# Re-ordering the loads and the work of the first batch element in a graph-network kernel

## The chip, the cores and the metric

The kernel runs on one core of a Trainium2 chip. The metric is the device time of one execution in microseconds (us). Before the change three runs took 2395.70, 2395.92 and 2396.19 us, median 2395.92 us. The profile is one further execution, of 2396.57 us, whose span from the first to the last instruction is 2394.8 us; the remaining 1.8 us lie outside the instructions.

## What is computed

There are 16 batch elements with 1024 nodes of 128 features and a 1024 x 1024 matrix `adj` each. Two residual blocks follow one another:

```python
# layer 0
degree = adj.sum(axis=-1)[:, :, None]
s   = einsum('bid,bij->bjd', x, adj) / degree
x   = layernorm(x + relu(concat([x, s]) @ W.T + b))
# layer 1: four GNN layers, each
src_agg = einsum('bjv,bij->biv', nodes @ ws + bs, adj / row_norms)
dst_agg = einsum('bjv,bji->biv', nodes @ wd + bd, adj / column_norms)
nodes   = tanh(concat([src_agg, nodes @ wn + bn, dst_agg]) @ wu + bu)
# then x = layernorm(x + nodes)
```

The norms are the square roots of the sums of squares of the rows and columns. Layers 2 and 3 read concatenated earlier features, so that their weights have two and three blocks of 128 rows.

## The kernel before, in words

Elements are worked off one after another (loop `for b in range(B)`, L1242). While TensorE multiplies for one element, the next one's matrix is loaded, squared, scaled and transposed beside it. This is possible for every element but the first, which has a stage of its own ahead of the loop (L1047 to L1236). The change touches that stage and the first pass of the loop (`if b == 0`).

The order of the instructions on each engine is the order of the program text (L1041 switches off any other scheduling). Each DMA issue is written on a named queue: `nc.sync` (the profile's SP), `nc.gpsimd` (POOL) or `nc.scalar` (ACT). Transfers of SP and ACT signal their landing on eight completion semaphores in rotation, so that an issue waits until the previous user of its semaphore has landed. POOL has eight of its own.

**Loads (L1063 to L1085).** `w0n` is the first layer's weight, `xn` holds x in two halves of nodes (h = 1 first), `a` the matrix in four "pairs" of row blocks (`PAIRS`), and each pair comes in four pieces, one for each group `g` of 32 partitions, 256 KB a piece. Before, SP issues `w0n`, groups 0 and 1 of both halves of x and groups 0 and 1 of all pairs; POOL issues groups 2 and 3 of all of them. SP then issues the small bias `b0c`, and for the four layers the weights (`fetch_weights`, L180) with four biases of 512 bytes each (L192), mixed with four blocks of transposed-to-be matrix rows (`load_rows`).

**First stage (L1182 to L1229).** TensorE transposes `w0` and x (`to_xT`), starts the sum of x and y in PSUM by a product of x with the identity (`with_x`), and multiplies x by its half of `w0` (`weights_of_x`). When a pair of row blocks has landed, `squares_of` takes the squares on ScalarE and the degrees on VectorE, and `gathers_of` makes four products of x with the matrix on TensorE. The sums are scaled (`scaled`), multiplied by the other half of `w0` and passed through relu into `yT` (`weights_of_agT`). `with_y` transposes y by products with the identity that accumulate onto x in PSUM. `norm_stats` reads that sum on VectorE and takes a power on GpSimd; half 1 is written by ScalarE (`norm_write_act`), half 0 by VectorE (`norm_write`), and `to_x1` transposes the result, a copy on ScalarE following.

Between these steps lie the weight foldings: since the layers are linear, `fold_begin` (transposes of three weights, their copies, and products of the biases) and `fold_end` (products of the transposed weights with `wu`, and their copies) merge `ws`, `wd`, `wn` with `wu`. They use two PSUM buffers in turn (`small`, L241), so a third waits for the copy of the first. Before, layer 0 and 1 are folded in the first stage, layer 1 with its transposes copied by VectorE and its bias copies held back (`biases`, L1222 and L1226) until ScalarE has written half 1 of the norm and copied its transpose.

**First layer of element 0 (L1259 to L1306).** `messages` makes four groups of products; functions in `between` are called after groups 0, 1, 2. `plain_layer` then makes 34 products of 512 columns: two of the node's own weights (`z`), sixteen with the matrix (`d`), sixteen with its transpose (`z`). `hooks` names what is issued ahead of which product. Before, layer 2 is folded at hooks 5 and 8, layer 3 at 9 and 12, and the sums of layer 2's weights are in `second0` at hook 11.

Of the kernel before, what the change touches and what calls it, by code (L numbers as in the profile page):

```python
# [8 lines left out]
F32 = mybir.dt.float32  # L9
# [5 lines left out]
P = 128  # L15
# [8 lines left out]
def adj_resnorm_kernel(ctx: ExitStack, tc: tile.TileContext, x, adj, w0, b0, layers, out):  # L24
# [152 lines left out]

        return wm if l in PAIRED else wm[:, :KEPT[l] * 2 * P].rearrange("p (c v) -> p c v", v=2 * P)

    def fetch_weights(raw, l, q, wm=None):  # L180
# [9 lines left out]
        bc = raw.take(4)  # L190
        for k, v in enumerate((bs, bd, bn, bu)):
            q.dma_start(bc[:, k:k + 1], v.rearrange("(p o) -> p o", o=1))  # L192
# [48 lines left out]
    def small(name, shape=(K,)):  # L241
        return ps_s.tile([P, *shape], F32, tag="small", name=name)
# [220 lines left out]
    def norm_stats(pn, blks, name, shifted=False):  # L463


        n = len(blks)
        stats = one.tile([P, BPH, 6], F32, tag="stats", name=f"st{name}")
        mv = two.tile([P, BPH, 2], F32, tag="mv", name=f"mv{name}")
        for q in range(n):
            nc.vector.bn_stats(stats[:, q], pn[:, blks[q]])  # L470
            nc.vector.bn_aggr(mv[:, q], stats[:, q])
        ve = two.tile([P, BPH], F32, tag="ve", name=f"ve{name}")
        nc.vector.tensor_scalar_add(ve[:, :n], mv[:, :n, 1], LN_EPS)
        rstd = two.tile([P, BPH], F32, tag="rst", name=f"rs{name}")
# [13 lines left out]
    def norm_write_act(dst, pn, stats, q):  # L488
        _, rstd, shift = stats
        nc.scalar.activation(dst, pn, AF.Identity, bias=shift[:, q:q + 1], scale=rstd[:, q:q + 1])  # L490
# [563 lines left out]
    def load_pair(q, pair, groups):  # L1054
        h, k = pair
# [3 lines left out]
    def load_nodes(q, h, groups):  # L1059
        for g in groups:  # L1060
            q.dma_start(xn[g * C:(g + 1) * C, h * BPH:(h + 1) * BPH], xv[h][g])

    nc.sync.dma_start(w0n, w0)  # L1063
    shares = ((nc.sync, range(G // 2)), (nc.gpsimd, range(G // 2, G)))
    for h in (1, 0):
        for q, groups in shares:
            load_nodes(q, h, groups)
    make_identity(nc, ident)
    for pair in PAIRS:
        for q, groups in shares:  # L1070
            load_pair(q, pair, groups)
    nc.sync.dma_start(b0c, b0.rearrange("(p o) -> p o", o=1))
    raw = Raw()
    wm = message_tile("wm1_0")
    Q = combined(0, "Q")
    places = {q: Q[i].rearrange("p k (u c) -> p (k u) c", u=2) for q, i in ((2, 2), (3, 3), (0, 4))}
    places[1] = one.tile([P, 2 * NJ, HW // 2], F32, tag="T2", name="rows1_0")
    rows, fetched = {}, []
    for l, q in enumerate((None, 2, 3, None)):
        fetched.append(fetch_weights(raw, l, nc.sync, None if l else wm))  # L1080
        if q is not None:
            rows[q] = load_rows(0, q, [places[q]])
    wm = as_chunks(wm, 0)
# [18 lines left out]
    pt = small("w0tr", [HW])  # L1102
    for k in range(2):
        nc.tensor.transpose(pt[:, k * P:(k + 1) * P], w0n[:, k * P:(k + 1) * P], ident)
    nc.scalar.copy(w0T.rearrange("p k v -> p (k v)"), pt[:, :2 * P])

    sq = []
    for p in (3, 4):
# [45 lines left out]
    def scaled(h):  # L1154
        nc.vector.tensor_mul(agT[:, half(h)], pa[h], dinv[:, half(h)])

    def weights_of_x(h):
        pw[h] = product(f"pw0_0_{h}")
        nc.tensor.matmul(pw[h], w0T[:, 0], xT[:, half(h)], start=True, stop=False)

    def weights_of_agT(h):
        nc.tensor.matmul(pw[h], w0T[:, 1], agT[:, half(h)], start=False, stop=True)
        nc.scalar.activation(blocks(yT[:, half(h)]), nodes(pw[h]), AF.Relu, bias=b0c)

    def with_x(h):

        pn[h] = ps_t.tile([P, BPH, P], F32, tag="pt", name=f"yn0_{h}")
        nc.tensor.matmul(pn[h].rearrange("p q d -> p (q d)"), ident, xn[:, h * BPH:(h + 1) * BPH].rearrange("p q d -> p (q d)"),
                         start=True, stop=False)

    def with_y(h):
        for q in range(BPH):
            i = h * BPH + q
            nc.tensor.matmul(pn[h][:, q], yT[:, i * P:(i + 1) * P], ident, start=False, stop=q == BPH - 1)

    def to_x1(h):
        pt = product(f"x1tr_{h}")
        for q in range(BPH):
            nc.tensor.transpose(pt[:, q * P:(q + 1) * P], x1n[:, h * BPH + q], ident)
        nc.scalar.copy(x1T[:, half(h)], pt)  # L1180

    for h in (1, 0):  # L1182
        to_xT(h)
        with_x(h)
        weights_of_x(h)
    for pair in PAIRS[:2]:
        squares_of(*pair)
        gathers_of(*pair)
    nc.vector.tensor_add(sq[6], sq[6], sq[7])
    add_square(5)  # L1190
    add_square(6)
# [1 line left out]
    degree_row(1)  # L1193
    squares_of(*PAIRS[2])
    gathers_of(*PAIRS[2])
    add_square(0)
    add_square(1)
    first, second = 2, 3
# [7 lines left out]
    gather(0, first)  # L1206
    weights_of_agT(1)
    square(first)
    square(second)
    gather(0, second)  # L1210
    add_square(first)
    with_y(1)
    scaled(0)
    weights_of_agT(0)
    stats = {1: norm_stats(pn[1], range(BPH), "0_0_1", True)}
    fold_begin(0, fetched[0])
    with_y(0)
# [12 lines left out]


    kept = scratch.tile([N, D], F32, tag="kept", name="kept0")
# [9 lines left out]
    for b in range(B):  # L1242
# [8 lines left out]
        if b == 0:  # L1251
# [13 lines left out]
            def rows0(destination, finish):  # L1265
                for q in (2, 3):
                    transpose_rows(rows[q], q, at)

            def cinv0(destination, finish):
                cinv[0] = factor_rows_now(0, 1, inv, "cinv")  # L1270

            def second0(destination, finish):
                columns0(range(NJ, NB), 1)
                sums_of_weights(2, fetched[2][3])
                weight_sums(own_seven(2, fetched[2][3]))
                nc.sync.dma_start(wsave[2], fetched[2][3])
                destination(1, cinv[0])
                columns0(range(NJ), 1)

# [380 lines left out]
```

## Time and profile before

| what | value |
|---|---|
| median of 3 runs | 2395.92 us |
| the profiled execution / its span | 2396.57 us / 2394.8 us |
| TensorE busy | 2377.7 us, 99% of the span |
| VectorE / ScalarE / GpSimd busy | 87% / 41% / 11% |
| TensorE clock granted | 1.0 throughout |
| first product with the matrix | at 13.31 us |
| first of the 34 products of element 0's first layer | at 42.45 us |

The page's shares of busy time are means over 2.4 ms, of which the changed stage is the first 60 us or so. To see that stage, ask for the busy times by stretches of time, then for the order of the instructions of one engine in such a stretch. In those rows the columns are start, duration, engine, line, operation, out<-in, shapes, count, and in brackets how long the engine was idle before and what ended it. Products in four-byte floats are two passes each, so 16 rows of `pa` are eight products.

### The profile page before, as it was taken

Reading aid. Unit: us, or ns where it says so; the run is one execution under the profiler, and the core shown is the slowest. Engines: PE = TensorE matmul, PEld = TensorE weight load, DVE = VectorE, ACT = ScalarE, POOL = GpSimd, SP = SyncE. Lnnn points to the kernel's source line nnn. Section 1 sums busy time; section 2 is a strip of 40 time slices with the busy share of each in tenths; the row PEclk is TensorE's granted clock in tenths of the full one; section 3 lists DMA queues with packets and bytes.
Section 4 is the critical chain, followed back from the end, with each engine's and each line's share of the span. In section 5 each row is a group of like instructions: output and inputs, shape, how many; then the busy total and the mean of one; then the engine's idle time right before and its main releaser. Section 6 shows DMA issues by size and latency. Waiting matters only on the chain.

```text
span 2394.8 us, 39324 instructions
## 1 busy us (share of the span) xinstructions
PE 2377.7 (99%) x15293; PEld 1288.4 (54%) x15293; DVE 2089.2 (87%) x2814; ACT 980.3 (41%) x1842; POOL 273.8 (11%) x102
## 2 busy tenths in 40 slices
PE   8999999999999999999999999999999999999998
PEld 4444554645556455554655546455464555645555
DVE  5998888999889989889988889888899888998954
ACT  5524345253343524435244452534525344352322
POOL 4101111001111011110111110111100111101110
PEclk9999999999999999999999999999999999999999
DMA  9527244262633627335272442634426253362400
GB/s 206 123 75 146 69 114 90 70 148 57 137 75 81 138 48 157 61 97 116 55 163 56 107 97 71 147 69 111 91 69 151 57 132 78 80 141 48 100 22 22
DMA packets 365897, 232.03 MB, mean 97 GB/s; under 512 B 152784, under 2 KB 336848, under 8 KB 365712
## 3 DMA queue, kind: packets, MB, share of 16 engines
q1 hardware_dynamic: 364944, 227.16, 42.6%
q0 software_dynamic: 768, 2.36, 0.4%
q8 instruction: 121, 1.98, 0.4%
q14 instruction: 64, 0.52, 0.1%
HBM read 209.59 MB, written 19.84 MB: 96 GB/s over the span
## 4 chain that ended last, share of the span: by engine, by line
PE 95%; DVE 2%; DMA 1%; SPq 1%; issue 1%; ACT 0%; POOLq 0%; DVEq 0%
PE m L1005 40%; PE z L1005 29%; PE pt L247 9%; PE pt_z L247 5%; PE m_f L583 5%; PE z_f L583 2%; PE pw L247 2%; PE m3s L1005 1%; PE z L851 1%; DMA wm<-in_L_gnn_ws_dram 1%; PE pt_p L247 1%; SPq L640 1%; DVE acc L331 0%; DMA a<-in_adj_dram 0%; PE d L851 0%
## 5 line engine op out<-in xcount | busy, mean ns | idle before, releaser
L1005 PE MATMUL m<-a,t 128*64 128x512 f32 x1008 | 434.6, 593 | 0.2 <-DVE t L711 0.2
L1005 PE MATMUL m<-at,t 128*64 128x512 f32 x1008 | 418.5, 592 | 0.0
L1005 PE MATMUL m<-Q,S 128*64 128x512 f32 x880 | 394.0, 593 | 0.0
L1005 PE MATMUL m<-T,S 128*64 128x512 f32 (+1 forms) x1040 | 393.5, 573 | 0.0
L456 POOL TENSOR_TENSOR rs<-ve,mhalf 128x32 f32<-128x32 f32 x30 | 191.9, 6396 | 987.9 <-DVE ve L454 987.9
L1005 PE MATMUL z<-at,t 128*64 128x512 f32 x504 | 229.2, 592 | 0.0
L1005 PE MATMUL z<-at,S 128*64 128x512 f32 x504 | 228.3, 593 | 0.0
L1005 PE MATMUL z<-a,S 128*64 128x512 f32 x504 | 228.2, 593 | 0.0
L1005 PE MATMUL z<-a,t 128*64 128x512 f32 x504 | 227.2, 593 | 0.0
L1005 PE MATMUL z<-Q,t 128*64 128x512 f32 x504 | 227.0, 593 | 0.0
L1005 PEld LDWEIGHTS m<-T,S 128*64 128x64 f32 x1040 | 131.0, 137 | 128.5 <-issue 126.5
L1005 PEld LDWEIGHTS m<-Q,S 128*64 128x64 f32 x880 | 118.2, 137 | 147.9 <-issue 141.0
L1005 PEld LDWEIGHTS m<-a,t 128*64 128x64 f32 x1008 | 131.9, 137 | 108.7 <-issue 100.0
L1005 PEld LDWEIGHTS m<-at,t 128*64 128x64 f32 x1008 | 131.3, 137 | 109.4 <-issue 108.0
L1005 PE MATMUL z<-T,t 128*64 128x512 f32 x384 | 172.8, 592 | 0.0
L884 ACT COPY e<-m 64x512 f32<-64x512 f32 x63 | 36.6, 582 | 327.9 <-PE m L1005 327.5
L376 POOL TENSOR_TENSOR inv<-cols,mhalf 128x16 f32<-128x16 f32 (+1 forms) x17 | 46.8, 2752 | 1031.2 <-DVE cols L375 1031.2
L414 DVE TENSOR_TENSOR a<-a,cinv 128x512 f32<-128x512 f32 x250 | 154.1, 694 | 1.9 <-ACT cinv L351 1.3
L322 ACT ACTIVATE sq<-a 128x1024 f32<-128x1024 f32 x120 | 125.9, 1050 | 37.1 <-DVE acc L329 23.2
L247 PE MATMUL pt<-wm,f1T 128*64 128x128 f32 (+1 forms) x1536 | 133.8, 309 | 0.0
L247 PEld LDWEIGHTS pt<-wm,f1T 128*64 128x64 f32 x1536 | 110.3, 137 | 31.9 <-issue 12.3
L317 ACT ACTIVATE a<-a 128x1024 f32<-128x1024 f32 x120 | 125.3, 1045 | 0.4
(302 smaller groups left out, 5019.8 us busy)
## 6 DMA issues: line engine op xcount, KB each, us to landing
a<-in_adj_dram SPq DMA_DIRECT2D x120, 512.0 KB, 12.3
rows<-in_adj_dram SPq DMA_DIRECT2D x480, 64.0 KB, 2.1
a<-in_adj_dram SPq DMA_DIRECT2D x240, 128.0 KB, 3.5
wm<-wsave SPq DMA_DIRECT2D x32, 704.0 KB, 5.0
wm<-wsave SPq DMA_DIRECT2D x31, 320.0 KB, 3.2
xn<-in_x_dram SPq DMA_DIRECT2D x124, 64.0 KB, 5.5
xs<-in_x_dram SPq DMA_DIRECT2D x60, 128.0 KB, 3.6
cinv<-dr SPq DMA_DIRECT2D x30, 256.0 KB, 6.4
```

The costliest lines, as they stand in the source:

```text
L247: nc.tensor.matmul(out[s], x[:, s], y, start=start, stop=stop)
L317: nc.scalar.activation(a[:, i, :], a[:, i, :], AF.Copy, accum_out=degree)
L322: nc.scalar.activation(sq, a[:, i, :], AF.Square, accum_out=state["cols"][:, i:i + 1])
L376: nc.gpsimd.tensor_tensor(inv[:, s], cols[:, s], mhalf[:, s], ALU.pow)
L414: engine.tensor_mul(a[:, i, s], a[:, i, s], cinv[:, s])
L456: nc.gpsimd.tensor_tensor(rstd, ve, mhalf[:, :n], ALU.pow)
L583: nc.tensor.matmul(o, x_, y_, start=start, stop=stop)
L640: nc.sync.dma_start(piece[g * C:(g + 1) * C, :, h * P:(h + 1) * P], v[h, g, :, k:k + n])
L851: nc.tensor.matmul(nodes(o) if len(y.shape) == 4 else o, x_, y, start=start, stop=stop)
L884: nc.scalar.copy(e0[high], A[high])
L1005: nc.tensor.matmul(o, x, y_, start=start, stop=stop)
```

## The change

Loads: SP issues all of x and most of the matrix; POOL only seven pieces of the matrix; the biases of layers 0 and 1 go to the ScalarE queue ahead of all else on it (`fetch_biases`). The weight `w0n` comes after the second pair's pieces on SP, and the second half of x after it. Layers 0, 1 and 2 have their weights fetched before the first block of rows.

TensorE starts with three products of a tile of zeros (`idle`), which VectorE fills. The transposes of `w0`, of x's second half and the products of x with `w0` come between the gathers. The sum of x and y is made on VectorE: `with_x` now transposes y into PSUM, adds `xn`, and writes `x1n`, from which the statistics are read.

ScalarE: the second of the last two squares comes after the second relu; `fold_begin(1)` and `fold_end(1)` run with all their copies on ScalarE before `norm_write_act`. The folding of layer 2 moves from hooks 5 and 8 into `messages`, and the sums of its weights from hook 11 to hook 6.

```diff
+    idle = one.tile([P, HW], F32, tag="S2", name="idle")
+    nc.vector.memset(idle, 0.0)
+    raw = Raw()
+    bcs = [raw.take(4) for _ in range(2)]
+    fetch_biases(nc.scalar, bcs[0], 0)
+    load_nodes(nc.sync, 1)
+    load_pair(nc.gpsimd, 0, (3,))
+    load_pair(nc.sync, 0, (0, 1, 2))
+    make_identity(nc, ident)
+    load_pair(nc.gpsimd, 1, (2, 3))
+    load_pair(nc.sync, 1, (0,))
+    fetch_biases(nc.scalar, bcs[1], 1)
+    load_pair(nc.sync, 1, (1,))
     nc.sync.dma_start(w0n, w0)
-    shares = ((nc.sync, range(G // 2)), (nc.gpsimd, range(G // 2, G)))
-    for h in (1, 0):
-        for q, groups in shares:
-            load_nodes(q, h, groups)
-    make_identity(nc, ident)
-    for pair in PAIRS:
-        for q, groups in shares:
-            load_pair(q, pair, groups)
+    load_nodes(nc.sync, 0)
+    load_pair(nc.gpsimd, 2, (2, 3))
+    load_pair(nc.gpsimd, 3, (2, 3))
+    load_pair(nc.sync, 2, (0, 1))
+    load_pair(nc.sync, 3, (0, 1))
...
-    for l, q in enumerate((None, 2, 3, None)):
-        fetched.append(fetch_weights(raw, l, nc.sync, None if l else wm))
+    for l, q in enumerate((None, None, 2, 3)):
+        fetched.append(fetch_weights(raw, l, nc.sync, None if l else wm, bcs[l] if l < 2 else None))
...
+    pt = product("idle")
+    for _ in range(3):
+        nc.tensor.matmul(pt, idle[:, :P], idle, start=True, stop=True)
...
     def with_x(h):
-        pn[h] = ps_t.tile([P, BPH, P], F32, tag="pt", name=f"yn0_{h}")
-        nc.tensor.matmul(pn[h].rearrange("p q d -> p (q d)"), ident, xn[:, h * BPH:(h + 1) * BPH].rearrange("p q d -> p (q d)"),
-                         start=True, stop=False)
-
-    def with_y(h):
+        pt = ps_t.tile([P, BPH, P], F32, tag="pt", name=f"yn0_{h}")
         for q in range(BPH):
             i = h * BPH + q
-            nc.tensor.matmul(pn[h][:, q], yT[:, i * P:(i + 1) * P], ident, start=False, stop=q == BPH - 1)
+            nc.tensor.transpose(pt[:, q], yT[:, i * P:(i + 1) * P], ident)
+        pn[h] = x1n[:, h * BPH:(h + 1) * BPH]
+        nc.vector.tensor_add(pn[h], pt, xn[:, h * BPH:(h + 1) * BPH])
...
-    for h in (1, 0):
-        to_xT(h)
-        with_x(h)
-        weights_of_x(h)
-    for pair in PAIRS[:2]:
-        squares_of(*pair)
-        gathers_of(*pair)
+    to_xT(1)
+    squares_of(*PAIRS[0])
+    gathers_of(*PAIRS[0])
+    transposes_of_w0()
+    squares_of(*PAIRS[1])
+    gathers_of(*PAIRS[1])
+    weights_of_x(1)
+    to_xT(0)
...
     gathers_of(*PAIRS[2])
+    weights_of_x(0)
...
     square(first)
-    square(second)
     gather(0, second)
     add_square(first)
-    with_y(1)
     scaled(0)
+    with_x(1)
     weights_of_agT(0)
     stats = {1: norm_stats(pn[1], range(BPH), "0_0_1", True)}
+    square(second)
     fold_begin(0, fetched[0])
-    with_y(0)
+    with_x(0)
     fold_end(0, fetched[0])
...
-    biases = fold_begin(1, fetched[1], nc.vector.tensor_copy, True)
-    for q in range(BPH):
-        norm_write_act(x1n[:, BPH + q], pn[1][:, q], stats[1], q)
-    to_x1(1)
-    biases()
+    fold_begin(1, fetched[1])
     fold_end(1, fetched[1])
     for q in range(BPH):
-        norm_write(x1n[:, q], pn[0][:, q], stats[0], q)
+        norm_write_act(pn[1][:, q], pn[1][:, q], stats[1], q)
+    to_x1(1)
+    for q in range(BPH):
+        norm_write(pn[0][:, q], pn[0][:, q], stats[0], q)
...
-            t = messages(b, 0, feats, wm, {0: lambda: to_x1(0), 2: row_factors0}, with_sums=False)
+            def second_x1():
+                to_x1(0)
+                fold_begin(2, fetched[2])
+
+            t = messages(b, 0, feats, wm, {0: second_x1, 1: lambda: fold_end(2, fetched[2]), 2: row_factors0},
+                         with_sums=False)
...
-            hooks = {4: lambda *_: inverses(0, st0, NB), 5: folded(2, fold_begin), 6: rows0, 7: cinv0,
-                     8: folded(2, fold_end), 9: lambda *_: fold_and_scale(3, 0), 11: second0, 12: folded(3, fold_end),
+            hooks = {4: lambda *_: inverses(0, st0, NB), 6: rows0, 7: cinv0,
+                     9: lambda *_: fold_and_scale(3, 0), 11: second0, 12: folded(3, fold_end),
```

More of the change, by code (lines that the diff above doesn't have):

```diff
@@ L178, in as_chunks, with fetch_biases, fetch_weights @@
         return wm if l in PAIRED else wm[:, :KEPT[l] * 2 * P].rearrange("p (c v) -> p c v", v=2 * P)
-    def fetch_weights(raw, l, q, wm=None):
+    def fetch_biases(q, bc, l):
+        for k, v in enumerate(layers[l][1::2]):
+            q.dma_start(bc[:, k:k + 1], v.rearrange("(p o) -> p o", o=1))
+    def fetch_weights(raw, l, q, wm=None, bc=None):
         ws, bs, wd, bd, wn, bn, wu, bu = layers[l]
@@ L189, in fetch_weights @@
         q.dma_start(wur, wu.rearrange("(c p) v -> p c v", p=P))
-        bc = raw.take(4)
-        for k, v in enumerate((bs, bd, bn, bu)):
-            q.dma_start(bc[:, k:k + 1], v.rearrange("(p o) -> p o", o=1))
+        if bc is None:
+            bc = raw.take(4)
+            fetch_biases(q, bc, l)
         if wm is not None:
@@ L1052, in adj_resnorm_kernel, with load_pair, load_nodes @@
     PAIRS = [(h, k) for h in (1, 0) for k in range(0, BPH, 2)]
-    def load_pair(q, pair, groups):
-        h, k = pair
+    def load_pair(q, i, groups):
+        h, k = PAIRS[i]
         for g in groups:
             q.dma_start(a[g * C:(g + 1) * C, h * BPH + k:h * BPH + k + 2], av[h][g, :, k:k + 2])
-    def load_nodes(q, h, groups):
-        for g in groups:
+    def load_nodes(q, h):
+        for g in range(G):
             q.dma_start(xn[g * C:(g + 1) * C, h * BPH:(h + 1) * BPH], xv[h][g])
-    nc.sync.dma_start(w0n, w0)
-    shares = ((nc.sync, range(G // 2)), (nc.gpsimd, range(G // 2, G)))
-    for h in (1, 0):
-        for q, groups in shares:
-            load_nodes(q, h, groups)
-    make_identity(nc, ident)
-    for pair in PAIRS:
-        for q, groups in shares:
-            load_pair(q, pair, groups)
+    idle = one.tile([P, HW], F32, tag="S2", name="idle")
[11 more added lines that the diff above has]
+    load_pair(nc.sync, 1, (1,))
+    nc.sync.dma_start(w0n, w0)
+    load_nodes(nc.sync, 0)
[3 more added lines that the diff above has]
+    load_pair(nc.sync, 3, (0, 1))
     nc.sync.dma_start(b0c, b0.rearrange("(p o) -> p o", o=1))
-    raw = Raw()
     wm = message_tile("wm1_0")
@@ L1100, in to_xT, with transposes_of_w0 @@
         nc.scalar.copy(nodes(xT[:, half(h)]), blocks(pt))
[L1102 to L1105, printed above, removed]
+    pt = product("idle")
+    for _ in range(3):
+        nc.tensor.matmul(pt, idle[:, :P], idle, start=True, stop=True)
+    def transposes_of_w0():
+        pt = small("w0tr", [HW])
+        for k in range(2):
+            nc.tensor.transpose(pt[:, k * P:(k + 1) * P], w0n[:, k * P:(k + 1) * P], ident)
+        nc.scalar.copy(w0T.rearrange("p k v -> p (k v)"), pt[:, :2 * P])
     sq = []
@@ L1267, in rows0 @@
                     transpose_rows(rows[q], q, at)
+                sums_of_weights(2, fetched[2][3])
+                weight_sums(own_seven(2, fetched[2][3]))
+                nc.sync.dma_start(wsave[2], fetched[2][3])
             def cinv0(destination, finish):
@@ L1273, in second0 @@
                 columns0(range(NJ, NB), 1)
-                sums_of_weights(2, fetched[2][3])
-                weight_sums(own_seven(2, fetched[2][3]))
-                nc.sync.dma_start(wsave[2], fetched[2][3])
                 destination(1, cinv[0])
```

## The prediction, made before the result

> **What bounds the kernel now.** I read the page's busy shares first, then the busy times by stretches of the first 82 us, then TensorE's and ScalarE's instructions in order, then the landings of the matrix pieces.
>
> ```profile
> PE 2377.7 (99%) x15293; PEld 1288.4 (54%) x15293; DVE 2089.2 (87%) x2814; ACT 980.3 (41%) x1842; POOL 273.8 (11%) x102
> ```
>
> TensorE is busy 99% of the span: 17 us are idle in all. A change to the first element can take only what is idle there, or move work into it.
>
> ```profile
> 0.00:13.30 13.30, 7.81 (x18) 3.79 (x19) 0.83 (x5) 2.83 (x5) 7.36 (x19) 1.00 0.83 222
> 13.30:26.06 12.76, 12.72 (x32) 5.58 (x33) 9.65 (x10) 8.08 (x15) 7.81 (x4) 1.00 0.88 204
> 26.06:36.87 10.81, 10.48 (x63) 7.43 (x61) 6.50 (x25) 7.43 (x18) 6.89 (x6) 1.00 0.90 177
> 36.87:42.45 5.58, 4.68 (x41) 2.57 (x41) 3.69 (x9) 1.96 (x7) 3.27 (x2) 1.00 0.94 174
> 42.45:62.48 20.03, 18.88 (x95) 11.94 (x94) 16.15 (x27) 15.28 (x42) 4.67 (x3) 1.00 1.00 223
> 62.48:81.46 18.98, 18.98 (x46) 8.18 (x44) 16.73 (x14) 4.45 (x11) 5.14 (x6) 1.00 0.93 222
> ```
>
> The columns after the stretch and its length are busy PE, PEld, DVE, ACT, POOL, the clock, the DMA share and GB/s. TensorE idles 5.49 us before 13.3, then 0.04, 0.33, 0.90 and 1.15 us, and nothing from 62.48 on. So whatever moves the products at 62.48 moves the end equally, as long as the later stages, which the change leaves alone, keep their distances.
>
> ```profile
> 4.34 0.69 PE L1104 MATMUL w0tr<-ident,w0n 128*128 128x128 f32 x2 [4.34 <-POOL ident masks.py:199]
> 5.98 1.91 PE L1168 MATMUL yn<-xn,ident 128*128 128x512 f32 x2
> 10.24 1.03 PE L1168 MATMUL yn<-xn,ident 128*128 128x512 f32 x2
> 13.31 7.11 PE L1132 MATMUL pa<-a,xn 128*128 128x512 f32 x16 [1.10 <-issue]
> 26.06 0.60 PE L359 MATMUL dinv<-ident,inv 128*128 128x128 f32 x4
> ```
>
> The gathers start at 13.31, when the first pair has landed, and run without a gap to 26.06; the first product with x took twice as long as the same one at 10.24.
>
> ```profile
> 31.26 0.69 ACT L1163 ACTIVATE yT<-pw,b0c 128x512 f32<-128x512 f32 x1
> 31.84 0.47 ACT L206 COPY raw<-wtr 128x384 f32<-128x384 f32 x1
> 33.86 0.37 ACT L229 COPY wm<-wm 128x256 f32<-128x256 f32 x1 [1.11 <-PE wm L227]
> 34.29 1.52 ACT L490 ACTIVATE x1n<-yn,sh,rs 128x128 f32<-128x128 f32 x4
> 36.23 0.59 ACT L1180 COPY x_T<-x1tr 128x512 f32<-128x512 f32 x1 [0.42 <-PE x1tr L1179]
> ```
>
> ScalarE writes half 1 of the norm as soon as layer 0's folding is copied. Its copy at 36.23 releases the messages at 36.87.
>
> [...] here the DMA share is 0.83 to 1.00 in every stretch, so the split brings an order, not bandwidth. [...] every row of ACT in the trace is in program order.
>
> **First pair.** The trace has the four pieces of the first pair landing at 8.2 and 9.3 (SP), 11.5 and 13.2 (POOL, issued 4.25 and 4.79, 7.3 and 8.4 us to landing). After, three pieces lie on SP behind 256 KB of x (384 KB before), and POOL's one piece is its first issue. SP had moved 1.04 MB by 7.5 us, and its pieces landed 2 us after their bytes were counted: 9.5. SP's fourth x load and the pieces now wait for ScalarE's bias transfers and earlier x to land (2.1 to 2.5 us each when the queues are idle at 25), which I estimate at 0.5. First gather: 10.0, bounds 8.5 and 11. That is 3.3 us earlier.
>
> **Work put behind it.** Products of x with `w0` (2 x 0.86), transposes of w0 (0.35) and of x's second half (0.55) leave the idle start. From first gather to `dinv_0`: 14 gathers at 0.86, 2.6 of these, one `dinv` at 0.45: 15.1 us, ending at 25.1. But the transposes of `w0` stand after the first pair's gathers, and `w0n` follows five pieces on SP: 1.70 MB, which SP had moved at 12.0, plus 2: 14.0 to 14.4. TensorE waits there from 13.4. From there on 11.7 us remain: 25.9 against 26.06. **Gain 0.15**, with bounds +2.5 (pair at 8.5, w0n at 12.0) and -1. The second pair (13.3) and the last (before 22.72, after about 21) are not later than that. The zero products, six passes of 0.85 from 1.4 to 6.5, lie in idle time and cost nothing; the two products of x with the identity go, 1.7 us, which the same idle time hid.
>
> **Sum on VectorE.** Four one-pass transposes replace eight passes for each half: -0.43 TensorE, twice, but TensorE waits for relu and `agT` at both places, so I count 0. The adds cost 2 x 0.69 (the price of L1155). Statistics of half 1 then end 0.4 late and GpSimd has its factors at 34.5; half 0's at 36.9 instead of 36.2. Both are needed only later, by what follows: 0.
>
> **ScalarE's order.** The relu stays at 31.26. Then, in line: square 1.15 to 33.1; wtr copy to 33.57; bias copies to 34.0 while TensorE makes `wm0` to 34.3; wm copies to 35.0; wtr of layer 1 0.47 to 35.5 (on VectorE before); its bias copies to 36.35; wm copies to 37.05; only now the norm, 1.52, to 38.57; transposes, copy to 39.6. The messages start at 39.65 instead of 36.87: **2.8 later**. Queued behind it are all of TensorE's messages; nothing covers it.
>
> **Layer 2's folding.** It takes TensorE 0.82 + 0.71 + 0.15 + 1.34, about 2.9 us, and waited 0.8 at hooks 5 and 8 (0.70 of it at 48.1 to 48.8, for ScalarE). In the messages it fills the 0.39 and 0.17 at 37.5 and 38.3 and waits some 0.3 itself for the copies: the first layer starts 7.75 after the messages instead of 5.58, +2.2, and later 3.7 fall away: **1.5 earlier**. The 0.9 us wait for `sp` at 40.4 stays, since `row_factors0` still follows its group.
>
> **VectorE's distance.** The layer loses 3.7 us on TensorE and none on VectorE, whose nine sums of weights (2.4 us) now fill its idle 1.30 at 51.7 and 0.67 at 57.8. At 74.70 it had 1.72 us to spare; I work out 0.5 too late there, so the second tanh and TensorE's third message group come 0 to 0.75 late. I take **+0.35**.
>
> **Sum.** -0.15 + 2.8 - 1.5 + 0.35 = +1.5 us. The profiled execution becomes 2398.1 (2396.57 + 1.5); the runs shown lie 0.65 lower at 2395.92, so 2397.4. Eight bias issues leave SP and the rows land earlier, but they had 5 us to spare (last row block 57.8, used 63.1), so this brings nothing. Element 1 and all after have the same instructions in the same order, since the order differs only in some 60 first rows of each engine.
>
> **Rivals.** (1) The loads are better than I reckon: first pair 8.5, w0n 12.0, VectorE in time. Then +2.5 instead of +0.15: -2.5 + 2.8 - 1.5 = -1.2, 2394.7. For it speaks that SP alone landed pieces 1 us apart at 8.2 and 9.3; against it that POOL now competes from the start. (2) The bias transfers hold the queue. `w0n` waits on SP for the landing of a 512-byte bias that ScalarE issues at about 3.3. Behind matrix pieces such a transfer took 13.7 us (`b0c`, 8.19 to 21.88) where an idle queue took 2.2. If it takes 13.7 here, it lands at 17.0, w0n at 19.2, and `dinv_0` starts at 30.9: 4.85 lost instead of 0.15 gained, together +6.5: 2402.4, slower by 0.27%. It decides from a bias landing after about 12. Against it: ScalarE's transfers have their own queue, and little is in flight at 3. (3) TensorE, idle from 6.7 to 10, goes cold again, and the first gathers take 6.8 instead of 3.4: 16.9 instead of 14.3, +2.6, 2400.0. [...] (4) The zero products do nothing, because TensorE is warm by the second pair anyway: no change to the sum.
>
> **How the numbers follow.** Faster or slower by over 0.2% is 4.8 us, about what a measurement of this kernel can tell from no change: below 2391.1 or above 2400.7. The sum as told: 0.60, 2395.5 to 2399.5. Rival 1: 0.18, down to 2394. Rival 2: 0.07. Rival 3: 0.09, of which a third with late loads lies above 2400.7. Something unseen: 0.06. So faster 0.03, same 0.86, slower 0.11. The range 2394.0 to 2401.0 leaves rival 2 and part of the rest out.
>
> **What would show it.** The first `pa` at 10 and `dinv_0` at 26; `w0tr` preceded by a wait for the w0n transfer; ScalarE's `x1n` at about 37, not 34, and the first `pt` at 39.7; the first `z` at 47.4 and the last stretch of 34 products without a gap, ending some 1.5 later than 81.46. I am wrong if `dinv_0` lies outside 23.5 to 27, or if the messages start within 1 us of their old distance from it.

## The result, and the profile after

The changed kernel takes 2408.5 us (median of 6 runs, 2408.11 to 2409.93) against 2396.51 us (6 runs of the kernel before beside them): ratio 1.005, 95% interval 1.0037 to 1.0062, 12 us slower. The forecast was 2397.4, within 2394.0 to 2401.0. The profiled execution's span is 2406.3 us, 11.5 more than before. Later runs of the kernel before had medians of 2396.16 to 2396.51; each ratio below is against the runs made beside it, and since these agree, medians of different series are compared as well.

The busy shares of the page:

```profile
PE 2381.8 (99%) x15287; PEld 1286.8 (53%) x15287; DVE 2089.5 (87%) x2816; ACT 981.0 (41%) x1843; POOL 272.2 (11%) x97
```

TensorE is busy 4.1 us longer, with six instructions fewer: it was idle some 7 us longer, and it was slower for a time. The busy times by stretches say where. The borders are the same events as before: the first gather (product of x with the matrix, rows `pa`), `dinv_0` (the second of the two `dinv` products, when all but two gathers are made; 26.06 before), the first message (rows `pt`) and the first `z`.

```profile
0.00:17.25 17.25, 6.12 (x11) 2.29 (x11) 1.28 (x6) 1.90 (x3) 4.70 (x14) 0.81 0.90 192
17.25:33.97 16.72, 16.72 (x42) 7.82 (x43) 9.52 (x10) 8.80 (x17) 8.62 (x4) 0.89 0.93 198
33.97:47.65 13.68, 10.50 (x55) 6.59 (x53) 7.43 (x28) 8.96 (x22) 8.76 (x7) 1.00 1.17 204
47.65:57.99 10.34, 9.36 (x65) 6.43 (x65) 2.96 (x6) 3.73 (x11) 0.58 (x1) 0.83 1.20 200
```

The second number of each row is the length of the stretch. Against before: 17.25 for 13.30 (+3.95), 16.72 for 12.76 (+3.96), 13.68 for 10.81 (+2.87), 10.34 for 5.58 (+4.76), and from the first `z` to the end of the span 2348.31 for 2352.35 (-4.04). That makes 11.5. The last column but two is the granted clock: 0.81, 0.89 and 0.83 where it was 1.00.

TensorE's instructions in order (brackets: idle before, and what ended it):

```profile
1.46 5.49 PE L1117 MATMUL idle<-idle 128*128 128x512 f32 x6 [1.46 <-DVE mhalf L1100]
8.86 0.63 PE L1112 MATMUL xtr<-ident,xn 128*128 128x128 f32 x4 [1.92 <-DMA xn<-in_x_dram]
17.25 5.49 PE L1150 MATMUL pa<-a,xn 128*128 128x512 f32 x8 [7.76 <-DMA a<-in_adj_dram]
22.58 0.38 PE L1122 MATMUL w0tr<-ident,w0n 128*128 128x128 f32 x2
22.79 3.60 PE L1150 MATMUL pa<-a,xn 128*128 128x512 f32 x8
```

The first pair's gathers start at 17.25 and not at the 10.0 forecast, after 7.76 us of idleness, and their eight passes take 5.49 where the next eight take 3.60. Such slow passes are called cold below, the others warm. `w0tr` waits for nothing, since `w0n` has landed by then (issued at 9.85, 10.0 us to landing).

The chain of waits, the first part of it, says what the first pair waited for:

```profile
2.15 4.51 DMA raw<-in_L_gnn_bu_dram
6.67 0.31 SPq L1061
6.99 0.04 issue
7.03 10.08 DMA a<-in_adj_dram
17.11 0.14 issue
17.25 5.49 PE pa L1150 x8
```

A bias of 512 bytes, issued by ScalarE at 2.15, lands 4.51 later. SP had to wait for it before it could issue the pair's second piece at 6.67, and the third at 7.03. That one takes 10.08 to land. Such a wait is in the kernel before too: `b0c`, the fourteenth issue on SP, went out at 8.19 after waiting 0.9 us, when the sixth, the first piece of the first pair, had landed (8.2). In the changed kernel, already the fourth load of x had waited 1.1 us for another bias, so that the first piece was issued at 3.50. SP's own waits list the 2.7 us ahead of the second piece (us in total, times, longest):

```profile
SPq L1061 <- DMA raw<-in_L_gnn_bu_dram: 2.7, 1, 2.7
```

What POOL did meanwhile, from its timeline:

```profile
1.32 0.75 POOL L1061 DMA_DIRECT2D a<-in_adj_dram  x1 [0.87 <-POOLq L1668]
2.62 3.16 POOL L1061 DMA_DIRECT2D a<-in_adj_dram  x6
```

All seven of its pieces, six of them for later pairs, were issued by 5.78, with no wait for a landing among them and ahead of SP's last two of the first pair.

ScalarE, in the order that the change gave it:

```profile
39.75 1.05 ACT L1137 ACTIVATE sq<-a 128x1024 f32<-128x1024 f32 x1
40.79 0.47 ACT L210 COPY raw<-wtr 128x384 f32<-128x384 f32 x1
...
44.95 1.65 ACT L494 ACTIVATE x1n<-x1n,sh,rs 128x128 f32<-128x128 f32 x4
47.01 0.59 ACT L1196 COPY x_T<-x1tr 128x512 f32<-128x512 f32 x1 [0.42 <-PE x1tr L1195]
```

The writing of the norm (`x1n`) now stands behind both foldings: from `dinv_0` to its start it is 10.98 us, where it was 8.23. The first messages follow at 47.65.

### The profile page after: what moved, and what is told of

Read it like the earlier page. It is cut to its first block, busy times and chain, and to the rows that moved or that the text cites. A ratio compares the mean times of both kernels' runs of the same rounds, so it can differ in the third digit from the quotient of the medians.

```text
span 2406.3 us, 39321 instructions
## 1 busy us (share of the span) xinstructions
PE 2381.8 (99%) x15287; PEld 1286.8 (53%) x15287; DVE 2089.5 (87%) x2816; ACT 981.0 (41%) x1843; POOL 272.2 (11%) x97
## 4 chain that ended last, share of the span: by engine, by line
PE 96%; DVE 2%; ACT 1%; DMA 1%; issue 1%; ACTq 0%; POOLq 0%; DVEq 0%; SPq 0%
PE m L1009 40%; PE z L1009 28%; PE pt L251 9%; PE pt_z L251 5%; PE m_f L587 5%; PE z_f L587 2%; PE pw L251 2%; PE pa L1150 1%; PE z L855 1%; PE m3s L1009 1%; PE pt_p L251 1%; PE d L855 0%; DMA a<-in_adj_dram 0%; DVE acc L335 0%; DMA raw<-in_L_gnn_bu_dram 0%
```

## The experiments

Each was timed beside runs of the kernel before on the same chip. The traces are of one execution each.

**Loads as before the change.** The changed kernel, with the old load block:

```diff
-    fetch_biases(nc.scalar, bcs[0], 0)
-    load_nodes(nc.sync, 1)
...
+    nc.sync.dma_start(w0n, w0)
+    shares = ((nc.sync, range(G // 2)), (nc.gpsimd, range(G // 2, G)))
+    for h in (1, 0):
+        for q, groups in shares:
+            load_nodes(q, h, groups)
```

> The changed kernel with the loads of the kernel before (x and every pair half on SP, half on POOL, biases on SP, weights and rows in the old order); the order of work on the engines is that of the changed kernel. Theory: of the 12 us, about 8 come from the loads alone. Then the first gather starts at about 13.3 instead of 17.25, dinv_0 at 26 to 28 instead of 33.97, and the time is about 2400.5 to 2402 (up to 1.3 of it a cold TensorE in the first pair, since the products with x no longer stand before it). Rival: the order of the work costs most of it and the loads only show it; then the time stays above 2405 although the first gather is at 13.3.

Measured: 2405.16 us, ratio 1.0035 (1.0022 to 1.0047). TensorE:

```profile
13.99 5.58 PE L1143 MATMUL pa<-a,xn 128*128 128x512 f32 x8 [6.22 <-DMA a<-in_adj_dram]
```

The first gather is nearly back (13.99), but only 3.3 us of the 12 are: `dinv_0` starts at 30.81 and not at 26 to 28. The first gathers are as slow as in the changed kernel, with 6.22 us of idle time ahead of them, and 2.4 us of work with w0 and x come between the later ones. The rival was right on the number: the order of the work costs more than half.

**Biases of layers 0 and 1 on SP again**, the rest as changed:

```diff
-    fetch_biases(nc.scalar, bcs[0], 0)
...
-    fetch_biases(nc.scalar, bcs[1], 1)
...
-        fetched.append(fetch_weights(raw, l, nc.sync, None if l else wm, bcs[l] if l < 2 else None))
+        fetched.append(fetch_weights(raw, l, nc.sync, None if l else wm))
```

> The changed kernel with the biases of layers 0 and 1 issued on SP after their weights again; the split of x and matrix between SP and POOL is that of the changed kernel. Theory A (SP's pieces of the first pair wait for the landing of ScalarE's biases, whose semaphores they share): the second piece is issued at about 4 instead of 6.67, the first gather starts at 12 to 13.5, dinv_0 at 27 to 29, the time is 2402 to 2404. Theory B (POOL's pieces of later pairs take the DMA engines [...]): the pieces are issued early but land late, first gather at 16 to 17, time 2406.5 to 2408.5.

Measured: 2403.69 us, ratio 1.0031 (1.0019 to 1.0043), 4.8 under the changed kernel.

```profile
12.40 6.10 PE L1147 MATMUL pa<-a,xn 128*128 128x512 f32 x8 [4.90 <-DMA a<-in_adj_dram]
```

SP issues its pieces of the pair at 2.60 to 3.55 and the gathers start 4.85 us earlier. First gather and time are those of theory A; `dinv_0`, at 29.73, is later than its 27 to 29, because the gathers are cold (6.10).

**The whole matrix on SP**, biases still on ScalarE's queue:

```diff
-    load_pair(nc.gpsimd, 0, (3,))
-    load_pair(nc.sync, 0, (0, 1, 2))
+    load_pair(nc.sync, 0, range(G))
...
-    load_pair(nc.gpsimd, 1, (2, 3))
-    load_pair(nc.sync, 1, (0,))
+    load_pair(nc.sync, 1, (2, 3, 0))
...
-    load_pair(nc.gpsimd, 2, (2, 3))
-    load_pair(nc.gpsimd, 3, (2, 3))
-    load_pair(nc.sync, 2, (0, 1))
-    load_pair(nc.sync, 3, (0, 1))
+    load_pair(nc.sync, 2, range(G))
+    load_pair(nc.sync, 3, range(G))
```

> The changed kernel with POOL's seven pieces of the matrix issued on SP as well, each pair whole and in order; the biases stay on ScalarE's queue. Theory B (POOL's pieces run ahead of SP's): with nothing on POOL, the first pair is the first 1 MB behind x, lands by about 13, first gather at 13, dinv_0 at 28 to 30, time 2403 to 2405, although SP still waits for biases. Theory A (the waits for the biases): the second piece is still issued at 6.7 or later, the first gather stays at 16 or later, time 2407 or more.

Measured: 2405.51 us, ratio 1.0036 (1.0023 to 1.0049). TensorE's first gathers, and below them SP's waits (us in total, times, longest):

```profile
12.38 5.45 PE L1146 MATMUL pa<-a,xn 128*128 128x512 f32 x8 [5.54 <-DMA a<-in_adj_dram]
```

```profile
SPq L1061 <- DMA raw<-in_L_gnn_bn_dram: 1.5, 1, 1.5
...
SPq L1061 <- DMA raw<-in_L_gnn_bu_dram: 0.3, 1, 0.3
```

Theory B's first gather came too: 12.38, although SP still waits for biases. The wait for `bu` ahead of the second piece shrinks from 2.7 to 0.3: without POOL's pieces that bias landed in 2.1 us instead of 4.5. So A and B aren't rivals: taking away either one moves the first gather by the same amount, 4.85 us. The time gains less (3.0) and stays just above theory B's range. One queue brings the later pairs late (0.54 and 0.24 of waits for the matrix at 24 and 28.8), and the stretch from the first message to the first `z` is 1.0 longer than in the changed kernel (11.35 for 10.34).

**Both on SP**: both edits at once.

> The changed kernel with the biases and all of the matrix on SP, nothing on ScalarE's and POOL's queues. Each of the two undoings alone brought the first gather to 12.4 from 17.25. If they remove the same delay (the product of both: slow biases because of POOL, waited for by SP), doing both brings little more than order: with one queue at some 200 to 230 KB per us from 2.5 on, x's half and four pieces, 1.3 MB, land at 10 to 11, and the last piece at 28, so that dinv_0 is at 29.5 to 31 and the time 2403 to 2405. If they were two separate delays of 4.85 each, the first gather would be at 7.6 to 9.

Measured: 2402.97 us, ratio 1.0024 (1.0014 to 1.0033).

```profile
9.93 5.37 PE L1143 MATMUL pa<-a,xn 128*128 128x512 f32 x8 [2.67 <-DMA a<-in_adj_dram]
...
21.40 3.67 PE L1143 MATMUL pa<-a,xn 128*128 128x512 f32 x8 [0.63 <-DMA a<-in_adj_dram]
```

First gather at 9.93: the forecast's 10.0, in a kernel with nothing on the other two queues. Together the two edits take away 7.3 us, and either one alone takes away 4.85. So 2.4 us (twice 4.85 less 7.3) are a common part, which needs both the biases and POOL's pieces; the rest of each is its own.

**Eight issues with one packet each.** ScalarE's issues stay, but fetch 512 bytes into one partition of an unused place; the biases in use come on SP.

```diff
-    bcs = [raw.take(4) for _ in range(2)]
-    fetch_biases(nc.scalar, bcs[0], 0)
+    lines = raw.take(P)
+
+    def fetch_lines(l):
+        for k, v in enumerate(layers[l][1::2]):
+            nc.scalar.dma_start(lines[4 * l + k:4 * l + k + 1], v.rearrange("(o p) -> o p", o=1))
+
+    fetch_lines(0)
...
```

> The changed kernel, but ScalarE's eight early issues fetch each bias as one line of 512 bytes into one partition of an unused place (one packet of data instead of 128 of four bytes); the biases that are used come on SP behind their weights, as before the change. So the eight issues, their landings and their share in the semaphores stay, and 1024 small packets become 8. Theory C [...]: the biases land within 3 us of their issue, SP's second piece is issued by 4, the first gather is at 12 to 13, the time 2403 to 2404.5, like the kernel with the biases on SP. Rival (the eight issues and the waits for their semaphores are what costs, whatever they carry): the second piece is still issued at 6 or later, first gather at 16 or later, time 2407 to 2409.

Measured: 2405.92 us, ratio 1.004 (1.0028 to 1.0053); the profiled execution, 2408.96, was the slowest of its five. TensorE, and SP's waits:

```profile
15.96 6.70 PE L1155 MATMUL pa<-a,xn 128*128 128x512 f32 x8 [8.99 <-DMA a<-in_adj_dram]
```

```profile
SPq L1061 <- DMA xn<-in_x_dram: 2.6, 2, 2.0
```

Neither expectation is met whole. The second piece is issued at 3.58, so the wait for biases is gone. But the eight issues still shift the rotation of the semaphores, and the third piece now waits 2.0 us for x's third load, until 5.98, when all of POOL's pieces have been issued. In the changed kernel that load landed at 6.12, so even without the slow bias the third piece would have waited until then. The profile lacks the landings of these biases, so how fast they were isn't known. The landing of the pair goes with the issue of its last piece (15.82 after 5.98, 17.11 after 7.03), whatever the wait before it was for.

**TensorE kept warm**: nine more products of zeros ahead of the first gather.

```diff
     to_xT(1)
+    pt = product("idle2")
+    for _ in range(9):
+        nc.tensor.matmul(pt, idle[:, :P], idle, start=True, stop=True)
```

> The changed kernel with nine more products of zeros (18 passes, about 7.7 us at 0.43) behind the transposes of x and ahead of the first gather; nothing else is changed. Theory: of the 12 us, about 2 are a cold TensorE: the eight passes of the first pair took 5.49 us instead of 3.43 after 7.76 us idle. Then they take about 3.45 here, the first gather still starts at 17.2, dinv_0 at 31.9 and the time is 2406.4. Rival: the clock is no part of it (the later pairs' landings set dinv_0 anyway): time unchanged at 2408.5.

Measured: 2409.4 us, ratio 1.0052 (1.0039 to 1.0065): no gain. By stretches (first gather to `dinv_0`; to the first message; to the first `z`):

```profile
18.05:32.95 14.90, 14.90 (x42) 7.11 (x43) 9.48 (x10) 8.80 (x17) 8.62 (x4) 1.00 0.95 193
32.95:46.78 13.83, 10.76 (x55) 6.68 (x53) 7.43 (x28) 8.96 (x22) 8.90 (x7) 0.93 0.92 189
46.78:57.88 11.10, 10.11 (x64) 6.94 (x65) 2.96 (x6) 3.72 (x11) 0.42 (x1) 0.77 1.20 192
```

The first stretch loses 1.82 us (14.90 for 16.72; the first eight passes take 3.67 for 5.49), and the gathers wait for no later pair, so the rival's reason is wrong. But the theory's time, 2406.4, isn't met either. In this execution the pair came 0.8 later, and a second slow spell, between the first message and the first `z`, is 0.76 longer (11.10 for 10.34). It was the fastest of the five; what held up the others isn't known.

**The norm first**: the changed kernel with layer 1's folding in its old order.

```diff
-    fold_begin(1, fetched[1])
-    fold_end(1, fetched[1])
+    biases = fold_begin(1, fetched[1], nc.vector.tensor_copy, True)
     for q in range(BPH):
         norm_write_act(pn[1][:, q], pn[1][:, q], stats[1], q)
     to_x1(1)
+    biases()
+    fold_end(1, fetched[1])
```

> The changed kernel with layer 1's folding as before the change: its transposes copied by VectorE, its bias copies and its second part behind the norm's half 1 and its transpose. The prediction priced the new order at 2.8. Theory: the messages start 2.8 earlier against dinv_0 (10.8 instead of 13.68), and the idle stretches that made TensorE run at half clock from 48 to 51 go, another 1: time 2404.5. Rival (the half clock comes from the cold start and not from these gaps, and the folding has to be done anyway): 2.8 at the messages, but 1 to 2 of it is lost again ahead of the first z: time 2406.5 to 2407.5.

Measured: 2405.57 us, ratio 1.0036 (1.0023 to 1.0048), 2.9 under the changed kernel, between the two expectations.

```profile
34.54 0.60 PE L363 MATMUL dinv<-ident,inv 128*128 128x128 f32 x4
...
45.98 1.08 PE L251 MATMUL pt<-wm,x_T 128*64 128x256 f32 x8
...
55.22 1.98 PE L855 MATMUL z<-x_T,wm 128*128 128x512 f32 x4
```

From `dinv_0` to the first message 11.44 (13.68 changed, 10.81 before): the folding's order is 2.24 of the 2.87. The other 0.63 is, by elimination, the second square behind the second relu; no run moves it alone. From there to the first `z` it is 9.24 for 10.34: the slow spell of 1.1 is gone with TensorE's waits for ScalarE (1.02 and 0.68 ahead of `x1tr` and the first message in the changed kernel), although the first gathers are as cold as before (5.56), so the rival's reason is wrong. The first gather of this execution was at 17.75, half a microsecond later than in the changed kernel's, and that hides some of the gain in its span.

One execution can't show that the waits cause the spell, but the profiled ones together point to it. Of the eight kernels with layer 1 folded ahead of the norm, seven have the spell and biases on SP hasn't; of the other six, none has it.

**Layer 2 ahead**: the kernel before, with only the move of layer 2's folding into the messages and of its sums to hook 6.

```diff
-            t = messages(b, 0, feats, wm, {0: lambda: to_x1(0), 2: row_factors0}, with_sums=False)
+            t = messages(b, 0, feats, wm, {0: second_x1, 1: lambda: fold_end(2, fetched[2]), 2: row_factors0},
+                         with_sums=False)
...
```

> The kernel before with only the move of layer 2's folding into the messages, and the sums of its weights to hook 6. The prediction had +2.2 ahead of the first z, 3.7 less behind it, and 0.35 for VectorE: -1.15, so 2395.2. Rival from the trace of the changed kernel (from the first message to the first z 9.2 to 11.3 instead of 5.58, 3.6 less later): 3.65 is paid ahead and 3.6 got back: no change, 2396.4.

Measured: 2396.59 us, ratio 1.0 (0.9992 to 1.0008), the rival's number.

```profile
37.59 1.08 PE L247 MATMUL pt<-wm,x_T 128*64 128x256 f32 x8
...
46.82 1.99 PE L851 MATMUL z<-x_T,wm 128*128 128x512 f32 x4
```

Between the two lie 9.23 us for 5.58 before: 3.65 paid. From the first `z` to the end of the span it is 2348.4 for 2352.35: 4.0 got back.

**Folding first**: the kernel before, with only ScalarE's order for layer 1 changed (the reverse of the edit under "The norm first").

> The kernel before with only ScalarE's order changed: layer 1 is folded whole, all copies on ScalarE, ahead of the norm's half 1. The prediction's price: messages 2.8 later against dinv_0, nothing that covers it: 2399.3. Rival: the gaps this opens on TensorE (about 0.75 + 0.3 + 1.0 + 0.7 within 8 us) let its clock fall to half, as in three of the earlier runs, so that another 1 to 2 is lost before the first z: 2400.3 to 2401.3.

Measured: 2399.38 us, ratio 1.0013 (1.0007 to 1.002), 3.2 above the kernel before.

```profile
36.90 1.38 PE L1179 MATMUL x1tr<-ident,x1n 128*128 128x128 f32 x4 [0.99 <-ACT x1n L490]
38.96 1.69 PE L247 MATMUL pt<-wm,x_T 128*64 128x256 f32 x8 [0.68 <-ACT x_T L1180]
```

`dinv_0` is at 25.92, so the first message comes 13.04 after it for 10.81: 2.23 for the order. The next ones are slow (granted clock 0.76 to the first `z`): 7.15 for 5.58, another 1.57. The median is the forecast's 2399.3, but not for its reason, since the order costs 2.23 of the 2.8 here and a slow spell comes on top. The 21 executions spread from 2397.49 to 2401.39 (2395.40 to 2398.47 in the kernel before), which would fit a spell in some and not in others; only one was traced.

**The sum on VectorE**: the kernel before, with only `with_x` and `with_y` changed.

```diff
     for h in (1, 0):
         to_xT(h)
-        with_x(h)
         weights_of_x(h)
...
```

> The kernel before with only the sum of x and y made on VectorE (transposes of y into PSUM, an addition, no products of x with the identity). The prediction counted 0: four one-pass transposes for eight passes, hidden behind waits: 2396.5. Rival: the two products of x with the identity kept TensorE busy until 11.7; without them it idles from about 9.5 to 13.3, goes cold, and the first pair's gathers take about 5.5 instead of 3.45: 2398.5.

Measured: 2398.72 us, ratio 1.0009 (1.0003 to 1.0016), 2.6 slower: the rival's number, but not its mechanism.

```profile
10.22 2.07 PE L1159 MATMUL pw<-x_T,w0T 128*128 128x512 f32 x2 [0.68 <-ACT x_T L1100]
13.68 9.05 PE L1132 MATMUL pa<-a,xn 128*128 128x512 f32 x16 [1.39 <-issue]
```

Sixteen passes take 9.05 for 7.11. The rival had TensorE cool down between 9.5 and 13.3. But at 10.22 it is still slow (2.07, for 1.10 in the kernel before), so without the two products with the identity it hadn't become warm at all. In the kernel before, they are the part of the work that makes it warm in time.

**Three things undone** in the changed kernel: loads and layer 1's folding as before, and seven more products of zeros ahead of the gathers (the edits above together).

> The changed kernel with three things undone: the loads and layer 1's folding as before the change, and seven more products of zeros behind the transposes of x so that TensorE doesn't cool ahead of the first gather. What stays of the change: work with w0 and x's second half behind the first gathers (2.4 us), the sum on VectorE, layer 2 folded in the messages. If the loads, the folding's order and the clock are all there is: first gather at 13.3 to 14, warm, dinv_0 at 28.2, first message 10.9 later, first z 9.2 after that, 3.6 got back: 2398 to 2399. If something else costs, it stays at 2400 or more.

Measured: 2398.93 us, ratio 1.0011 (1.0005 to 1.0018). The same stretches:

```profile
13.45:28.35 14.90, 14.90 (x42) 7.10 (x43) 9.52 (x10) 8.81 (x17) 8.62 (x4) 1.00 0.78 186
28.35:39.80 11.45, 10.01 (x56) 6.49 (x54) 7.84 (x29) 7.56 (x18) 6.54 (x6) 1.00 1.00 197
39.80:49.03 9.23, 7.84 (x65) 5.38 (x65) 3.00 (x7) 4.34 (x15) 2.82 (x2) 1.00 1.02 198
```

As expected: `dinv_0` at 28.35 for 28.2, and the time in the range. The loads, the folding's order and the clock carry 9.6 of the 12 us. The rest is the work put between the gathers (14.90 for 12.76) and the 0.64 of the second stretch (11.45 for 10.81), while layer 2's folding, 3.65 later at the first `z`, is got back.

**A balanced version** that might have beaten both: x's first half and the first pair ahead of all else, half on SP and half on POOL, four more products of zeros, the foldings as before.

```diff
+    for q, groups in shares:
+        load_nodes(q, 1, groups)
+    for q, groups in shares:
+        load_pair(q, 0, groups)
     make_identity(nc, ident)
...
+    for q, groups in shares:
+        load_pair(q, 1, groups)
     nc.sync.dma_start(w0n, w0)
...
```

> A version that might beat both: loads split half and half over SP and POOL as before, but only x's first half ahead of the first pair, and w0 and x's second half behind the second; biases on SP; layer 1 and layer 2 folded as before the change; the sum on VectorE; four more products of zeros between the transposes of x and the first gather. If transfers land in the order of their issue over both queues at about 1 us for 256 KB, the first pair lands at 9.5 to 10.5, and with 14.9 us of work behind it dinv_0 is at 25.2 against 26.06: 2395 to 2396.5. Rival: as in the changed kernel, the work put behind the gathers (2.4) takes back what the earlier pair gives, or the later pairs are late: 2397 to 2399.

Measured: 2398.37 us, ratio 1.0008 (1.0 to 1.0017): the rival.

```profile
11.87 3.67 PE L1148 MATMUL pa<-a,xn 128*128 128x512 f32 x8 [0.30 <-issue]
...
21.18 3.67 PE L1148 MATMUL pa<-a,xn 128*128 128x512 f32 x8 [0.25 <-DMA a<-in_adj_dram]
```

The gathers begin 1.4 us before those of the kernel before, but what was moved behind them takes 2.4, another 0.25 goes on a wait for the matrix, and `dinv_0` is at 27.26 for 26.06. No version here beats the kernel before.

## Why the prediction was wrong

**The step that failed first: "SP had moved 1.04 MB by 7.5 us, and its pieces landed 2 us after their bytes were counted: 9.5", with 0.5 for the biases, "First gather: 10.0".** It was 17.25. The working is right for SP alone: with nothing on the other queues it was 9.93. The step counted only SP's own bytes and put the waits for the biases at 0.5; they made the third piece 3.48 us later (7.03 for 3.55 with the biases on SP). And the pieces that SP had issued then stood behind POOL's. From 10 to 12 us of the changed kernel, with two SP pieces of the first pair issued at 6.67 and 7.03, the queues moved (packets, MB, share of the 16 DMA engines; q0 is POOL's, q10 ScalarE's, SP's would be q1):

```profile
q0 software_dynamic: 126, 0.42, 106.2%
q10 hardware_dynamic: 2, 0.00, 0.1%
```

Not one packet was SP's. So the landing goes with what both queues had been given by the time the pair's last piece was issued. From the issues and landings in the traces, the last piece of the first pair:

| kernel | issued, us | KB issued up to and with it, SP and POOL | landed, us |
|---|---|---|---|
| both on SP | 4.01 | 1280 | 9.79 |
| balanced | 3.15 | 1792 | 11.78 |
| biases on SP | 3.55 | 1792 | 12.26 |
| before | 4.79 | 2176 | 13.22 |
| one packet | 5.98 | 2816 | 15.82 |
| changed | 7.03 | 2816 | 17.11 |

An estimate fitted to this table, 2.9 us (about where the first transfers land) plus 1 us for each 200 KB, gives 9.3, 11.9, 11.9, 13.8, 17.0 and 17.0: within 1.2 us of each. The matrix on SP alone is an exception (1280 KB, 12.24 for 9.3): there SP's waits for biases held its last piece until 5.11, so less was in flight before (DMA share 0.61 from 5 to 8 us). Without the biases the gathers would have come at 12.4, 2.4 later than forecast, since POOL's first pieces share the way (12.40 with biases on SP, 9.93 with POOL's pieces on SP as well). The waits for the biases then let POOL put all its seven ahead, another 4.85.

A bias took 4.5 us where the forecast had 2.1 to 2.5 "when the queues are idle". POOL's pieces have a part in it: the wait for `bu` was 2.7 with them in flight and 0.3 without, and its landing took 4.5 and 2.1. How they hold it back stays open: no run here separates a bias waiting its turn behind POOL's packets from any other delay of its landing.

**Rival 2** had the mechanism (SP waits for ScalarE's bias) and put it at `w0n`, the price being 6.5 in all. It happened earlier in the queue, at the first pair itself, where 3.48 us of later issue cost 4.85 at the first gather.

**Rival 3**, "TensorE, idle from 6.7 to 10, goes cold again", priced at 2.6, came true with 7.76 us of idleness. It cost 1.82 us, as the kernel kept warm shows (14.90 for 16.72 in the same stretch). A slow spell came a second time where no step looked for it, right after TensorE's waits for ScalarE between 44 and 48: the messages and foldings from 47.65 on cost 1.1 more than in the runs without a spell (10.34 for 9.24 with the norm first; granted clock 0.83 for 1.00). The waits alone don't decide it: biases on SP has the same ones (1.02 and 0.68) and no slow spell (9.23), the whole matrix on SP one of 2.1 (11.35). What decides whether a spell comes and how long it lasts, no run here shows.

**"The two products of x with the identity go, 1.7 us, which the same idle time hid", cost nothing:** wrong by about 2 us in the kernel before, as the sum on VectorE shows there: they were the warm-up. In the changed kernel this is the cold start just counted. The three products of zeros that replace them run from 1.46 to 6.95, and with the pair at 17.25 that is too early to keep TensorE warm for it (5.49 for the first eight passes, 3.60 for the next). Rival 4 (they do nothing) had this outcome, with another reason; no run leaves them out.

**The wait for `w0n`** (0.8) didn't occur; the pair came too late for it. From the first gather to `dinv_0` the rest of the working held: 15.1 forecast, 14.90 measured without the cold start.

**ScalarE's order, 2.8:** right for the changed kernel as a whole. 13.68 - 10.81 = 2.87, of which the norm first took back 2.24.

**Layer 2's folding, +2.2 and -3.7, with 0.35 for VectorE:** the second term was right (-4.0 to the end of the span, so VectorE cost nothing), the first too small. It was 3.65 in undisturbed stretches, 1.45 more. Some 0.4 of that is arithmetic: the step's own terms, 2.9 of work less 0.56 filled plus 0.3 of waiting, give 2.6 and not 2.2. Another 0.56 is idle time that wasn't there: the step filled "the 0.39 and 0.17 at 37.5 and 38.3", but the row it had quoted for that stretch, 4.68 busy of 5.58, leaves 0.90 idle, which is the wait for `sp` alone (0.89). The rest is somewhat more work (3.1 for 2.9) and waiting. The move is worth nothing.

**The sum.** What the forecast left out, in us: first gather 7.25, cold start 1.82, messages 1.45, second slow spell 1.1, together 11.6. What it had too much: the wait for `w0n` (0.8), 0.2 between the gathers, and 0.7 behind the first `z`. With 0.07 for ScalarE's order that is 10.0 net, and 1.5 + 10.0 is the measured 11.5. The largest error by far is the first. It isn't the only one that matters: had the first gather come at 10.0, the time would be an estimated 2402 (2408.5 less 7.25, plus the 0.8), still above 2401.0, and the kernel with both on SP, whose first gather was at 9.93, took 2402.97.

## What to carry to other kernels

Estimate a transfer's landing from what all queues have been given before it is issued, not from its own queue alone (the estimate from both queues is within 1.2 us of the six kernels in the table, the count on SP alone was 7.25 off). Treat a wait for a tiny transfer as a possible wait for the large ones around it (512 bytes took 4.5 us with POOL's pieces in flight, 2.1 without). Issue what is needed first ahead of what is fetched early for later, also on other queues. Work that lies in idle time can be what keeps TensorE fast (without the two products with the identity the first gathers took 9.05 for 7.11), so look at the duration of the next products before calling its removal free. Of a move, check that the idle time it is to fill is idle time of the engine that gets the work.

## What was not expected of the hardware

Here one queue alone didn't reach the rate of two. The first row is from 8 to 10 us with all on SP, the second from 12 to 14 in the kernel before, with SP and POOL (last columns: clock, DMA share, GB/s):

```profile
8.00:10.00 2.00, 0.07 (x1) 0.10 (x1) 0.09 (x1) 0.10 (x1) 0.00 (x0) 1.00 1.03 201
```

```profile
12.00:14.00 2.00, 0.90 (x3) 0.48 (x3) 0.70 (x1) 0.71 (x1) 0.00 (x0) 1.00 1.04 303
```

The DMA share is nearly the same, the bytes are half as many again, in 256 KB pieces of the same matrix. With all on SP it was 207 to 221 from 16 to 24 us too, so the first row is no exception. So the prediction's "an order, not bandwidth", read from the DMA share, doesn't hold for these two queues when both carry pieces of the matrix. From 10 to 12 us of the changed kernel, when only POOL's pieces moved, it was 209. The balanced version, where SP and POOL issue `w0n` and x's second half behind the second pair, stayed at 229 to 238 from 12 to 16 with both. Why a single queue is slower wasn't tried.

The granted clock in the profile doesn't show every slow spell: with the sum on VectorE it reads 1.00 from 0 to 28 us, while the first gathers took 9.05 for 7.11. In the kernel before it also reads 1.00 from the start, while the product with x at 5.98 took 1.91 and the same one at 10.24 took 1.03.
